# A graph layer on one core: load order, residual bias, scatter inputs and first-edge columns rearranged

## The chip, the cores and the metric

The kernel runs on one core of a Trainium2 chip. The metric is the device time of one execution in microseconds (us); lower is better. A core has TensorE (PE, with its weight loads listed apart as PEld), VectorE (DVE), ScalarE (ACT), GpSimd (POOL) and SyncE (SP), each with its own queue of instructions that run in order, and DMA queues that SP, ACT and POOL issue to. DRAM is the chip's large memory; all engines compute on the on-chip memory.

## The reference

One layer of a graph network with 625 nodes of 512 features, 20625 edges (10000 in both directions and a loop at each node, sorted by destination) and 4 relations. All is float32.

```python
h = relu(layernorm(x))                                  # x: 625 x 512
xs = h[src]
for r in range(4):
    w_r = where(edge_type == r, edge_weight, 0)
    total_msg += (xs @ W_rel[r] + b_rel[r]) * w_r[:, None]
agg = segment_sum(total_msg, dst) / maximum(segment_sum(edge_weight, dst), 1)
x1  = layer_norm(h + h @ W_self + b_self + agg, ln1)
ffn = gelu(x1 @ W_ffn1 + b_ffn1) @ W_ffn2 + b_ffn2      # 512 -> 1024 -> 512
out = x + layer_norm(x1 + ffn, ln2)
```

## The kernel before

The nodes lie in five blocks of 128 rows. One function, `gnn_layer`, holds everything as nested helpers, and its work falls into two phases.

**Phase 1** builds a table in DRAM with one row for every pair of node and relation: h of the node times W_rel, scaled and with b_rel added. The loop `for r in range(R)`, `for i in range(NB)` makes 20 steps; step c = 5 r + i calls `table_rows(r, i)` (L393): four products of 128x512 on PE (L402), one VectorE operation that scales and adds the bias (L415) into a tile called m or tr, and a store by SP (L417). Step 19 is cut in two, 384 and 128 columns, with an operation and a store each. The normalized blocks come from `x_stats` (L372) and `pre_norm` (L364), and ACT copies their transposes (`transposed`, L353). The inputs are loaded by SP in the order of the lines from L262 on: x in xs, the first relation's weights in wr, the line of edges that reach the first outer block (`load_line`), the biases.

Beside this stand three pieces of preparation, hung into the steps. (1) The edges of the two outer blocks (0 and 4) are taken as lines: `line_columns` and `line_sums` (L631, L666, VectorE) add up the weights of equal edges and give a column of weights and a column of places (tiles weight and cell); `scatter` (L684) sends one such column into a DRAM array, cells, by an indirect DMA of POOL (L685) with a short memset behind it. `load_sums` (L702, a DMA of ACT's queue at L705) reads such an array back as sums_w, 1280 KB, after all its scatters. PE then multiplies sums_w with table rows kept on chip or read back (tr): the chunk products of L1290. (2) Further edges of the outer blocks are handled through one-hot matrices: `node_hots` (L577) makes os (L580) and od (L590) on VectorE, `weighted_hots` (L594) makes ohw from os on ACT (L598), and `outer_sum` (L612) multiplies ohw and od on PE. The first three groups, `pre_hots`, are made in steps 15 to 17; there are three ohw buffers (191, 192, 193). (3) The first edges of the inner blocks' nodes are fetched into x_edges, and `first_columns` (L802) turns them with 17 small VectorE operations into rows to gather (x_row), weights (x_on) and degrees (rdeg).

At the end of phase 1 POOL adds the bias of the last layer, b2, to x in place (L1105, five blocks); the last normalization adds that xs to its output. Then the memory pool `early` is closed. The tiles of the pool `edge`, opened next, lie where those of `early` lay: eight ms buffers, es, oh and ow. So a first write to one of them waits for what last read the old tile beneath it, scatters among them.

**Phase 2** gathers table rows edge by edge: `gather` (L1143) issues an indirect DMA of POOL (L1145) into one of the eight ms buffers and a memset (L1148) as a pause, 99 times; `gather_first` does six more (L1203). In front of the first stands `after_stores` (L699), a memset on POOL (L700) that waits for the stored rows 0 to 18 and for every scatter; the two stores of row 19 are waited for by the first gather itself. ACT (L1152) and VectorE (L1170) weight and add the rows of one destination, and `edge_sum` multiplies the sums with a one-hot of the destinations, oh (L1181, four operations with two scalars each), on PE: L1195 in one float32 product, or L1192 and L1193 with a sum split in eh and el. The first tiles go straight from ms to PE. For each block follow the first normalization, the feed-forward part (`up` L917, gelu on ACT L921, `down` L935), the second normalization and the store (L986). PE products into `spin` (L1214) fill waits.

The order of phase 2 on each engine comes from a list planner, `Plan` (L76). Every operation is given to it with an engine, an assumed duration, what it comes after, the buffers it takes and gives back, a rank and a level; the planner simulates the engines and emits the operations in the order of its simulated times. The instructions then run in that order on their engine, with semaphore waits for their real inputs. Phase 1 is emitted in the order of its code.

## Time and profile before

| | us |
|---|---|
| median of 3 runs | 267.01 (266.51 to 267.12) |
| the profiled execution | 267.43 |
| its span in the trace | 265.5 |
| PE busy | 248.5 (94%) |
| POOL busy | 200.8 (76%) |
| DVE busy | 198.3 (75%) |
| ACT busy | 64.5 (24%) |

Times in the trace count from the start of the span. A row of a timeline gives start, duration, engine, line, operation, output tile <- input tiles with shapes and a count, and in brackets how long the engine idled before it and what ended that wait. Rows with SPq, ACTq or POOLq are the issue of a DMA by that engine. A group's row gives busy time in all, the mean in ns, and the idle time ahead. A float32 product of 128x512 appears as two records. Lines are those of the kernel before.

### The profile page before, as it was taken

What the parts mean: (1) busy time and instruction counts of PE and PEld (TensorE: products, weight loads), DVE (VectorE), ACT (ScalarE), POOL (GpSimd) and SP (SyncE); (2) the same over time, 40 slices, a digit from 0 to 9 for tenths busy, and PEclk for the clock granted to TensorE, in tenths of its full rate; (3) what the DMA queues carried; (4) which work ended last, traced back from release to release, by engine and by line L of the source; (5) the groups of instructions that cost most, each with busy time, mean ns of one, the idle gap of its engine ahead of it and who ended that gap; (6) DMA issues with size and microseconds to landing.
All of it is one profiled execution on the core that took longest, in us unless ns stands there. A gap on an engine that the chain in (4) does not pass through costs nothing.

```text
span 265.5 us, 3627 instructions
## 1 busy us (share of the span) xinstructions
PE 248.5 (94%) x1055; PEld 142.0 (53%) x1055; DVE 198.3 (75%) x493; ACT 64.5 (24%) x148; POOL 200.8 (76%) x408
## 2 busy tenths in 40 slices
...
GB/s 208 350 408 408 393 359 339 299 271 80 93 267 83 310 256 258 213 369 292 324 316 327 266 200 196 199 197 197 184 197 215 204 191 233 200 81 1 43 0 42
DMA packets 23848, 60.20 MB, mean 227 GB/s; under 512 B 4321, under 2 KB 8673, under 8 KB 22674
## 3 DMA queue, kind: packets, MB, share of 16 engines
...
q14 instruction: 13, 0.11, 0.1%
HBM read 50.77 MB, written 9.17 MB: 226 GB/s over the span
## 4 chain that ended last, share of the span: by engine, by line
POOL 26%; PE 24%; DVE 23%; DMA 15%; issue 7%; ACT 1%; SPq 1%; POOLq 0%; DVEq 0%; ACTq 0%
POOL ms L1145 15%; DMA ms<-table,row_i 11%; PE ps L935 8%; POOL cells L685 5%; PE ps L917 4%; PE acc L1195 4%; PE ps L402 3%; POOL zeros L1148 3%; DVE tr L415 3%; DMA wr<-in_L_gnn_W_rel_dram 3%; DVE add L1170 2%; DVE same L671 2%; DVE oc L764 2%; DMA cells<-weight,cell 2%; PE spin L1214 1%
## 5 line engine op out<-in xcount | busy, mean ns | idle before, releaser
L1145 POOL DMA_INDIRECT ms<-table,row_i x99 | 100.1, 1011 | 15.9 <-issue 12.7
L402 PE MATMUL ps<-wr,hT 128*128 128x512 f32 (+2 forms) x168 | 71.0, 576 | 1.9 <-DMA wr<-in_L_gnn_W_rel_dram 1.9
L685 POOL DMA_INDIRECT cells<-weight,cell x43 | 45.6, 1061 | 9.4 <-issue 5.6
L402 PEld LDWEIGHTS ps<-wr,hT 128*128 128x128 f32 x168 | 30.6, 190 | 35.7 <-issue 32.2
L1170 DVE SCALAR_TENSOR_TENSOR add<-ms,wgt_g,add 128x512 f32<-128x512 f32 x40 | 29.9, 750 | 17.1 <-DMA ms<-table,row_i 15.0
L917 PEld LDWEIGHTS ps<-x1T,w_sb 128*128 128x128 f32 x320 | 37.7, 192 | 6.8 <-issue 4.1
L917 PE MATMUL ps<-x1T,w_sb 128*128 128x128 f32 (+1 forms) x320 | 38.2, 275 | 1.9 <-ACT gT L921 1.9
L1152 ACT ACTIVATE add<-ms,ed 128x512 f32<-128x512 f32 x30 | 20.7, 691 | 72.0 <-DMA ms<-table,row_i 54.5
L935 PE MATMUL ps<-w_sb,gT 128*128 128x512 f32 (+3 forms) x96 | 35.9, 522 | 0.0
L598 ACT ACTIVATE ohw<-os,w 128x128 fp32r<-128x128 f32 x40 | 12.4, 388 | 66.6 <-DVE os L580 66.6
L1290 PE MATMUL acc<-tr,sums_w 128*128 128x512 f32 x60 | 28.2, 595 | 0.3 <-PE ps L440 0.3
L935 PEld LDWEIGHTS ps<-w_sb,gT 128*128 128x128 f32 (+1 forms) x96 | 16.6, 188 | 15.8 <-issue 12.6
L1195 PE MATMUL acc<-es,oh 128*128 128x512 f32 x40 | 20.9, 603 | 2.5 <-DVE es L1170 2.5
L1148 POOL MEMSET zeros<- 128x100 bf16 x99 | 19.9, 201 | 0.1
L440 PE MATMUL ps<-ws_sb,hT 128*128 128x512 f32 x40 | 18.3, 592 | 0.0
L1290 PEld LDWEIGHTS acc<-tr,sums_w 128*128 128x128 f32 x60 | 11.1, 190 | 13.2 <-issue 11.7
L921 ACT ACTIVATE gT<-ps,bf 128x128 f32<-128x128 f32 (+1 forms) x40 | 13.7, 363 | 18.0 <-PE ps L917 14.9
L1170 DVE SCALAR_TENSOR_TENSOR es<-ms,wgt_g,add 128x512 f32<-128x512 f32 x20 | 14.9, 743 | 3.2 <-DMA ms<-table,row_i 3.0
L415 DVE SCALAR_TENSOR_TENSOR tr<-ps,rx,brel_bc 128x512 f32<-128x512 f32 x15 | 11.2, 745 | 4.1 <-POOL idle L688 2.1
L612 PE MATMUL ps<-od,ohw 128*128 128x260 f32 (+13 forms) x40 | 11.1, 405 | 2.3 <-ACT ohw L598 2.3
L440 PEld LDWEIGHTS ps<-ws_sb,hT 128*128 128x128 f32 x40 | 7.5, 190 | 9.1 <-issue 9.1
L1195 PEld LDWEIGHTS acc<-es,oh 128*128 128x128 f32 x40 | 6.9, 189 | 8.1 <-DVE es L1170 4.3
...
## 6 DMA issues: line engine op xcount, KB each, us to landing
...
ms<-table,row_i POOLq DMA_INDIRECT x99, 3.8
rows<-in_rows_dram SPq DMA_DIRECT2D x1, 1536.0 KB, 13.2
```

Of the source, the lines that this page charges most:

```text
L402: nc.tensor.matmul(p_[:, :h.stop - h.start], hT[i][:, k, :], wr_sb[r][:, k, h], start=(k == 0), stop=(k == KD - 1))
L415: nc.vector.scalar_tensor_tensor(m[:, h], p_[:, :h.stop - h.start], rx[:, i, 1:2], brel_bc[:, r * D + h.start:r * D + h.stop], op0=ALU.mul ...
L440: nc.tensor.matmul(p[0], hT[i][:, k, :], ws_sb[:, k, :], start=(k == 0), stop=(k == KD - 1))
L685: s = nc.gpsimd.indirect_dma_start(out=cells[i][:, :], out_offset=bass.IndirectOffsetOnAxis(ap=cell[i][:, k:k + 1], axis=0), in_=weight[i] ...
L917: nc.tensor.matmul(pu[:, :nn], w1_sb[:, k, f * P:(f + 1) * P], x1T_b()[:, k, :nn], start=(k == 0), stop=(k == KD - 1))
L935: nc.tensor.matmul(po[h][:n, :w], box["gT"][:, f, at], w2_sb[:, f, c], start=(f == 0), stop=(f == KF - 1))
L1145: nc.gpsimd.indirect_dma_start(out=ms[j], out_offset=None, in_=table[:, :], in_offset=bass.IndirectOffsetOnAxis(ap=row_i[:, j:j + 1], axis=0))
L1148: nc.gpsimd.memset(zeros[:, :PAUSE // 2], 0.0)
L1152: nc.scalar.activation(box["sum"], ms[j], AF.Copy, scale=wgt[:, j:j + 1])
L1170: nc.vector.scalar_tensor_tensor(to, ms[j], wgt_g[:, k, q - 1:q], box["sum"], op0=ALU.mult, op1=ALU.add)
L1195: nc.tensor.matmul(acc[bs], ohs[0][:, q, :].bitcast(F32), box["sum"] if "sum" in box else ms[j], start=(k == 0), stop=last)
L1290: nc.tensor.matmul(acc[b,], sums_w[b][:, c, :], kept[(b, c) if (b, c) in kept else c], start=first, stop=last)
```

## The change

Four edits. (1) In the queue of SP, the second quarter of the first relation's weights goes ahead of the second block of x, and the rest of them ahead of the line of edges. (2) The five additions of b2 to xs go from POOL, at the end of phase 1, to VectorE: two in step 16, two in step 17, one in step 18, each behind that step's L415. (3) The tiles weight and cell, which the scatters read, are taken from a pool (`mid`) that stays open, so that no tile of phase 2 lies on them, and `after_stores` waits for the stored rows alone. (4) `first_columns` is cut into `first_rows` (6 operations, which wait for the last L415), `first_found` (5) and `first_degrees` (6). The gathers of first rows wait for `first_rows` only, the additions that use rdeg or x_on for the last step; the planner is given 1.2 us and level 0.2 for each in place of 2.4 us and level 1.5 for the whole.

```diff
@@ line 262 of before
     nc.scalar.dma_start(xs[:, 0, D // 2:], x[:P, D // 2:])
     nc.sync.dma_start(xs[:, 0, :D // 2], x[:P, :D // 2])
     load_wr(0, [(0, 1)])
+    load_wr(0, [(1, 2)])
     load_x(1, 2)
-    load_wr(0, [(1, 2)])
+    load_wr(0, [(2, 4)])
     load_line(0)
-    load_wr(0, [(2, 4)])
     load_x(2, 3)
     load_rows(brel_bc[:, :D], 0, D)
     load_x(3, NB)
@@ line 388 of before
     held = range(NL - LA * CH, NL)
     kept = {}
 
-    stored = []
+    stored, made_row = [], []
 
     def table_rows(r, i, between=None):
         c = r * NB + i
@@ line 412 of before
                 kept[OUTER[0], c] = m
         row0 = r * NP + i * P
         for p_, h in zip(p, at):
-            nc.vector.scalar_tensor_tensor(m[:, h], p_[:, :h.stop - h.start], rx[:, i, 1:2],
-                                           brel_bc[:, r * D + h.start:r * D + h.stop], op0=ALU.mult, op1=ALU.add)
+            made_row.append(nc.vector.scalar_tensor_tensor(m[:, h], p_[:, :h.stop - h.start], rx[:, i, 1:2],
+                                           brel_bc[:, r * D + h.start:r * D + h.stop], op0=ALU.mult, op1=ALU.add).ins)
             stored.append(nc.sync.dma_start(table[row0:row0 + P, h], m[:, h]).ins)
 
     begun = set()
@@ line 619 of before
         nc.gpsimd.iota(spill[-1], pattern=[[1, n]], base=P * NC * P, channel_multiplier=n,
                        allow_small_or_imprecise_dtypes=True)
         for of, name in ((place, "place"), (found, "found"), (weight, "weight")):
-            of.append(early.tile([P, n], F32, name=f"{name}_{b}"))
-        cell.append(early.tile([P, n], I32, name=f"cell_{b}"))
+            of.append((mid if name == "weight" else early).tile([P, n], F32, name=f"{name}_{b}"))
+        cell.append(mid.tile([P, n], I32, name=f"cell_{b}"))
         line_f.append(early.tile([P, 3, n + 2 * NEAR + 1], F32, name=f"line_f{b}"))
         line_key.append(early.tile([P, n + 2 * NEAR + 1], F32, name=f"line_key{b}"))
 
@@ line 697 of before
                               reason=reason)
 
     def after_stores():
-        wait_for(nc.gpsimd.memset(idle[:, :2], 0.0), [*stored[:NC - 1], *sum(scattered, [])], "rows are stored")
+        wait_for(nc.gpsimd.memset(idle[:, :2], 0.0), stored[:NC - 1], "rows are stored")
 
     def load_sums(i):
         b = lines[i][0]
@@ line 799 of before
                 out=x_edges[:, b, :, :].rearrange("p q f -> p (q f)"), out_offset=None, in_=edge_groups[:, :],
                 in_offset=bass.IndirectOffsetOnAxis(ap=x_group[:, b:b + 1], axis=0))
 
-    def first_columns():
-
-        nc.vector.tensor_copy(x_cols, x_edges[:, :, :, 0:3])
+    def first_rows():
+
+        wait_for(nc.vector.tensor_copy(x_cols, x_edges[:, :, :, 0:3]), made_row[-1:], "behind the last row")
         for f in range(2):
             nc.vector.tensor_scalar(x_step, x_cols[:, :, :, f], float(ep.gap_at), float(ep.gap), op0=ALU.is_ge, op1=ALU.mult)
             nc.vector.tensor_add(x_cols[:, :, :, f], x_cols[:, :, :, f], x_step)
         nc.vector.scalar_tensor_tensor(x_row, x_cols[:, :, 1:, 2], float(NP), x_cols[:, :, 1:, 0], op0=ALU.mult, op1=ALU.add)
+
+    def first_found():
+
         of_node = xw[:, 0, :]
         nc.vector.tensor_tensor(x_on, x_cols[:, :, 1:, 1], of_node.unsqueeze(2).to_broadcast([P, INNER, EG - 1]),
                                 op=ALU.is_equal)
@@ line 813 of before
         nc.vector.tensor_mul(x_on, x_on, xw[:, 2, :].unsqueeze(2).to_broadcast([P, INNER, EG - 1]))
         nc.vector.reduce_sum(x_found, x_on.rearrange("p b q -> p (b q)"), axis=mybir.AxisListType.X)
         nc.vector.tensor_sub(x_missing, x_missing, x_found)
+
+    def first_degrees():
+
         nc.vector.tensor_mul(x_on, x_on, x_edges[:, :, 1:, 3].bitcast(F32))
         nc.vector.reduce_sum(x_deg, x_on, axis=mybir.AxisListType.X)
         nc.vector.tensor_add(rdeg[:, 1:NB - 1], rdeg[:, 1:NB - 1], x_deg)
@@ line 998 of before
     WARM = 24
     ES = 8
     LAND = 3.6
-    HOTS_AT, SELF_AT = (15, 16, 17), 15
+    HOTS_AT, SELF_AT, ADDS_AT = (15, 16, 17), 15, (16, 17, 18)
     OHS = 3
     OW = 5
     GT = 2
@@ line 1077 of before
                     cols = degree_columns()
                 if step in DEGREE_HOTS_AT:
                     hots.append((step, degree_hots(*chunks[DEGREE_HOTS_AT.index(step)], *cols)))
+                if step in ADDS_AT:
+                    for b in range(*((0, 2), (2, 4), (4, NB))[ADDS_AT.index(step)]):
+                        nc.vector.tensor_add(xs[:, b, :], xs[:, b, :], b2_bc)
                 if step == SELF_AT:
                     for k in range(KD):
                         w_k = ws_sb[:, k, k * P:(k + 1) * P]
@@ line 1101 of before
                     total_outside = count_outside()
             later_loads(r)
         assert not columns
-        for b in range(NB):
-            nc.gpsimd.tensor_add(xs[:, b, :], xs[:, b, :], b2_bc)
         assert not pieces and len(DEGREE_HOTS_AT) == len(chunks)
     early_stack.close()
     edge = ctx.enter_context(tc.tile_pool(name="edge", bufs=3))
@@ line 1123 of before
     op = todo.op
     at_ = {}
 
-    first_ready = op("DVE", 2.4, first_columns, rank=(0.3,), level=1.5)
+    rows_of_first = op("DVE", 1.2, first_rows, rank=(0.3,), level=0.2)
+    first_ready = op("DVE", 1.2, first_found, after=[rows_of_first], rank=(0.3,), level=0.2)
+    first_ready = op("DVE", 1.2, first_degrees, after=[first_ready], rank=(0.3,), level=0.2)
 
     def read_outside():
         at_["outside"] = nc.values_load(n_out[0:1, 0:1], min_val=0, max_val=4 * P * NT)
@@ line 1228 of before
         for b in range(1, NB - 1):
             if bs == ((b, b + 1) if b < NB - 2 else (b,)):
                 for q in range(EG - 1):
-                    g_last = op("POOL", GATHER, lambda b=b, q=q: gather_first(b, q, ms), after=[g_last, first_ready],
+                    g_last = op("POOL", GATHER, lambda b=b, q=q: gather_first(b, q, ms), after=[g_last, rows_of_first],
                                 take=["ms"], lag=LAND, order=True, rank=(0, n))
-                    adds[b].append(op("DVE", 0.75, lambda b=b, q=q: add_first(b, q, ms), after=[g_last],
+                    adds[b].append(op("DVE", 0.75, lambda b=b, q=q: add_first(b, q, ms), after=[g_last, first_ready],
                                       give=[("ms", g_last)], lag=SLACK, rank=(0.3, n), level=0.05))
         for k, unit in enumerate(units):
             box, needs, got = {}, [], []
@@ line 1276 of before
         for q, b in enumerate(bs):
             half_ = slice(0, P) if len(bs) == 1 else slice(H, P) if q == 0 else slice(0, H)
             m = op("DVE", 0.72, lambda b=b, bs=bs, half_=half_: add_to(b, lambda: acc[bs], half_),
-                   after=[m], give=["acc"] if b == bs[-1] else [], rank=(0.3, n), level=1.5 if len(bs) == 1 else 0.05)
+                   after=[m, first_ready], give=["acc"] if b == bs[-1] else [], rank=(0.3, n), level=1.5 if len(bs) == 1 else 0.05)
             adds[b].append(m)
 
     def chunk_load(b, c, n):
@@ line 1339 of before
             op("PE", 0.1, read_outside, after=[t, m[b]], rank=(2, 2.365))
     for b in OUTER:
         adds[b].append(op("DVE", 0.72, lambda b=b: add_to(b, lambda: acc[b,], slice(0, P)),
-                          after=[m[b]], give=["one"], rank=(0.4,)))
+                          after=[m[b], first_ready], give=["one"], rank=(0.4,)))
 
     turned = {}
     sums_done = {}
```

The changed kernel's lines from L804 on stand 6 to 9 higher: L1290 is L1299 there, L1195 is L1204, L917 is L923, L935 is L941. Beside the planner's figures the edits change what the planner orders, on PE and ACT too. On ACT, around the end of phase 1, where cells_98 and cells_100 are the two arrays of scattered sums and the sums_w tiles what is read back from them, stood:

```order
L598 ACTIVATE ohw_191<-os_844,w_159 128x128 x4
L705 DMA sums_w_877<-cells_98 128x2560
L598 ACTIVATE ohw_192<-os_879,w_159 128x128 x4
L598 ACTIVATE ohw_193<-os_894,w_159 128x128 x4
L705 DMA sums_w_988<-cells_100 128x2560
L598 ACTIVATE ohw_191<-os_997,w_159 128x128 x4
L598 ACTIVATE ohw_192<-os_1004,w_159 128x128 x4
```

and stands now:

```order
L598 ACTIVATE ohw_191<-os_844,w_159 128x128 x4
L705 DMA sums_w_877<-cells_98 128x2560
L598 ACTIVATE ohw_192<-os_881,w_159 128x128 x4
L705 DMA sums_w_977<-cells_100 128x2560
L598 ACTIVATE ohw_193<-os_898,w_159 128x128 x4
L598 ACTIVATE ohw_191<-os_981,w_159 128x128 x4
L598 ACTIVATE ohw_192<-os_990,w_159 128x128 x4
```

The second load, which waits for the last scatters, went from behind the third group of ohw (193) to ahead of it.

On PE, between the first group of products with gathered tiles (its last one reads ms_941) and the second (ms_942 to ms_945), where od and ohw are the one-hots of the outer blocks and sums_w the scattered sums, stood:

```order
L1195 MATMUL acc_2_1034<-ms_941,oh_958 128x512
L612 MATMUL ps_79<-od_190,ohw_193 128x240 x2
L1290 MATMUL acc_954<-tr_734,sums_w_877 128x512
L1290 MATMUL acc_954<-m_837,sums_w_877 128x512
L612 MATMUL ps_79<-od_188,ohw_192 128x240 x2
L1195 MATMUL acc_2_1102<-ms_942,oh_1059 128x512
L1195 MATMUL acc_2_1102<-ms_943,oh_1059 128x512
```

and stands now:

```order
L1204 MATMUL acc_2_1041<-ms_941,oh_970 128x512
L612 MATMUL ps_79<-od_190,ohw_193 128x240 x2
L612 MATMUL ps_79<-od_188,ohw_192 128x240 x2
L612 MATMUL ps_79<-od_189,ohw_192 128x220 x2
L612 MATMUL ps_80<-od_1_185,ohw_191 128x480
L612 MATMUL ps_80<-od_1_185,ohw_191 128x220
L612 MATMUL ps_80<-od_187,ohw_191 128x200 x2
L1299 MATMUL acc_954<-tr_734,sums_w_877 128x512
L1299 MATMUL acc_954<-m_837,sums_w_877 128x512
L1299 MATMUL acc_954<-m_874,sums_w_877 128x512
L1204 MATMUL acc_2_1123<-ms_942,oh_1066 128x512
L1204 MATMUL acc_2_1123<-ms_943,oh_1066 128x512
```

Six products of od more and one more chunk product (m_874) stand ahead of the product with ms_942.

On PE at the end of phase 2, around the last two products with gathered sums (acc_1), the up products (x1T) and down products (gT) of the block before and the transposes of the last block (ow), stood:

```order
L1195 MATMUL acc_1_1774<-es_1974,oh_1827 128x512
L917 MATMUL ps_81<-x1T_1848,w_sb 128x128 x4
L917 MATMUL ps_79<-x1T_1848,w_sb 128x128 x4
L935 MATMUL ps_78<-w_sb,gT_1920 128x512 x2
L1195 MATMUL acc_1_1774<-es_2000,oh_1946 128x512
L1195 MATMUL acc_1_1774<-ms_938,oh_1984 128x512
L935 MATMUL ps_78<-w_sb,gT_1920 128x512 x6
L350 MATMUL ps_80<-ident,ow_950 128x128 x2
L350 MATMUL ps_81<-ident,ow_950 128x128 x2
L1214 LDWEIGHTS zeros
```

and stands now:

```order
L923 MATMUL ps_81<-x1T_1855,w_sb 128x128 x4
L941 MATMUL ps_80<-w_sb,gT_1922 128x512 x4
L1204 MATMUL acc_1_1779<-es_2009,oh_1953 128x512
L1204 MATMUL acc_1_1779<-ms_945,oh_1991 128x512
L941 MATMUL ps_80<-w_sb,gT_1922 128x512 x4
L1223 LDWEIGHTS zeros
L1223 MATMUL spin<-zeros 128x256
```

followed by four more such pairs of spin and then by the transposes. Two down products went ahead of the last two sums, and the five spins ahead of the transposes instead of behind.

## The prediction

> **What bounds the kernel now.** I read the page first: the line of engines under the chain of work that ended last, and the costliest groups.
>
> ```profile
> POOL 26%; PE 24%; DVE 23%; DMA 15%; issue 7%; ACT 1%; SPq 1%; POOLq 0%; DVEq 0%; ACTq 0%
> L1145 POOL DMA_INDIRECT ms<-table,row_i x99 | 100.1, 1011 | 15.9 <-issue 12.7
> ```
>
> No engine holds the chain by itself. POOL leads with the gathers of phase 2: 99 of 1.011 us (six more stand at L1203), each with a 0.2 us memset behind it, and nearly all idle time ahead of them is "issue". The table by stretches (length, then busy PE, PEld, DVE, ACT, POOL with their counts, the clock, the DMA share and GB/s) shows whether they ever wait.
>
> ```profile
> 100.00:230.00 130.00, 123.21 (x502) 71.46 (x501) 100.35 (x205) 41.66 (x86) 114.64 (x191) 1.00 0.77 239
> ```
>
> POOL is busy for 115 of these 130 us, and the rest is the 0.16 us ahead of each gather that the row above calls "issue". So the stream never waits; when it starts decides when it ends. Does its end set the kernel's end? The timeline there:
>
> ```profile
> 227.56 0.69 ACT L1152 ACTIVATE add<-ms,ed 128x512 f32<-128x512 f32 x1 [4.47 <-DMA ms<-table,row_i]
> 228.59 2.05 PE L917 MATMUL ps<-x1T,w_sb 128*128 128x128 f32 x16 [1.39 <-ACT gT L921]
> 230.75 1.14 POOL L1145 DMA_INDIRECT ms<-table,row_i  x1 [0.16 <-issue]
> 237.03 5.31 PE L935 MATMUL ps<-w_sb,gT 128*128 128x512 f32 x12
> ```
>
> At 227.56 ACT has waited 4.47 us for a gather; the gelu queued behind that add lets PE go on at 228.59, after 1.39 us of idling. From there PE is busy through the last row sum, which ends as 237.03 begins, and on. So the gathers hold the end through ACT, and PE has 1.39 us of slack there. **Model: the end moves with the stream's start, unless PE comes later than those 1.39 us allow.** The turn between the phases starts the stream:
>
> ```profile
> 81.27 4.14 DMA cells<-weight,cell
> 82.33 6.18 POOL L1105 TENSOR_TENSOR xs<-xs,rows 128x512 f32<-128x512 f32 x5
> 88.71 1.01 POOL L1145 DMA_INDIRECT ms<-table,row_i  x1
> ```
>
> The last scatter is issued at 81.27 and lands 4.14 us later, at 85.4 (this row is of the chain of waits); from 82.33 POOL adds, to 88.51; the memset at L700, whose stores and scatters are all done by then, and the first gather follow. The adds alone set 88.71.
>
> **The change part by part.** Everything is set against the profiled execution, 267.43 us around a span of 265.5; the runs' median, 267.01, is 0.42 lower.
>
> *Adds off POOL.* POOL would be free at 82.4. What is late next? The gathers read the table, so all its stores must have landed. The rows of the tile table between 60 and 90 us give that, the last for its stores from issue to landing:
>
> ```profile
> L417 SPq DMA_DIRECT2D table<-m x6: 319/320/320, 70.4 to 84.5; - x6
> DMA to landing us min/median/max: 1.9/2.3/4.9
> ```
>
> The last store is issued at 84.5. The bounds are 1.9 and 4.9, the latter the store of row 16, beside which the first load of sums (1280 KB) ran. I take 1.9, since the last store is the smallest (64 KB) and nothing so large is in flight: 84.5 + 1.9 = 86.4, the first gather starts there instead of at 88.71. Term: **-2.3**; bounds -2.3 and +0.7 (84.5 + 4.9 = 89.4).
>
> *Adds on VectorE.* Their price is that of an addition of the same shape, beside the L415 rows of phase 1's end:
>
> ```profile
> L885 DVE TENSOR_TENSOR z<-ow,rows 128x512 f32<-128x512 f32 x5 | 3.4, 687 | 0.0
> 77.20 0.75 DVE L415 SCALAR_TENSOR_TENSOR m<-ps,rx,brel_bc 128x512 f32<-128x512 f32 x1 [1.71 <-PE ps L402]
> 80.64 0.75 DVE L415 SCALAR_TENSOR_TENSOR m<-ps,rx,brel_bc 128x512 f32<-128x512 f32 x1
> 83.22 0.62 DVE L415 SCALAR_TENSOR_TENSOR m<-ps,rx,brel_bc 128x384 f32<-128x384 f32 x1 [1.83 <-PE ps L402]
> 84.11 0.35 DVE L415 SCALAR_TENSOR_TENSOR m<-ps,rx,brel_bc 128x128 f32<-128x128 f32 x1 [0.27 <-PE ps L402]
> ```
>
> Five times 0.687 is 3.4 us. Step 16's two (1.37) lie in the 1.71 us that DVE idled before 77.20. Step 17's two push row 18's L415 from 80.64 to about 82.0; its store follows, and landing the median 2.3 later it is there by 85.2, ahead of row 19's. Step 18's one lies in the 1.83 us before 83.22. The last L415 waits for PE at 84.11, with or without them. Term: **0**; without that cover, the 1.37 of step 17 at most.
>
> *Scatter inputs in memory of their own.* Here the old wait takes DVE's time too:
>
> ```profile
> 84.37 2.31 PE L612 MATMUL ps<-od,ohw 128*128 128x460 f32 x12
> 85.80 0.33 ACTq L705 DMA_DIRECT2D sums_w<-cells  x1
> 85.83 3.53 DVE L1181 TENSOR_SCALAR oh<-node_row,dst_mod,ed 128x128 f32<-128x128 f32 x4 [1.37 <-DMA cells<-weight,cell]
> L1181 DVE TENSOR_SCALAR oh<-node_row,dst_mod,ed x8: 334/340/2762, 85.8 to 97.5; 128x128 f32<-128x128 f32 x8
> 89.29 0.17 DVE L804 CAST x_cols<-x_edges 128x27 f32<-128x27 int32 x1
> 92.81 4.78 ACT L598 ACTIVATE ohw<-os,w 128x128 fp32r<-128x128 f32 x16 [13.20 <-DVE os L580]
> 93.26 1.46 PE L612 MATMUL ps<-od,ohw 128*128 128x500 f32 x4 [2.29 <-ACT ohw L598]
> ```
>
> DVE waited 1.37 us for the scatters, then took 3.53 us for four operations because one lasted 2762 ns against 340 (POOL's adds ran), then did the first columns, 17 operations from 89.29 to 92.3; only then came os, at 92.7, and ACT and PE starved behind it. After, DVE goes on at 84.5: six of the 17 (1.1), the four oh at 0.34 (1.3, with their gaps), os at about 86.9. PE's 2.29 us are over, but ACT is late next: the order puts the load that waits for every scatter ahead of ohw_193. That load left at 85.80, for 0.33; behind it the four weightings of ohw_193 run at 0.30 to 0.35 us each (16 in 4.78), to 87.5. Four of the twelve products that PE does from 84.4 need them, and PE has the eight others done at 85.7. So PE stalls about 1.1 us there (the first is ready at 86.5, the rest pace at 0.32 instead of the 0.19 of 2.31 over 12). Net -1.2.
>
> The idle gap had a second price, which the table shows in the column of the clock:
>
> ```profile
> 94.00:97.00 3.00, 2.95 (x6) 1.64 (x7) 2.98 (x11) 3.00 (x12) 2.68 (x5) 0.50 0.86 296
> 97.00:98.00 1.00, 1.00 (x5) 0.53 (x3) 1.00 (x5) 1.00 (x5) 0.84 (x2) 0.88 0.70 188
> 228.00:229.00 1.00, 0.41 (x3) 0.41 (x4) 0.71 (x1) 1.00 (x4) 0.88 (x1) 1.00 0.64 160
> ```
>
> After 2.29 us of idling the granted clock was 0.50 for 3 us and some tenths, which cost some 1.6 us; at the 1.39 us of idling at 228 it was 1.00. A stall of 1.1 should leave it, so PE gains 1.2 + 1.6 = 2.8 us in all (bounds: nothing, with a stall like the old one, and 3.9 without any). That is more than the stream's 2.3. Does the new order of products hold a buffer too long?
>
> ```profile
> 102.46 3.60 PE L1195 MATMUL acc<-ms,oh 128*128 128x512 f32 x8
> 105.73 0.95 POOL L1145 DMA_INDIRECT ms<-table,row_i  x1 [0.16 <-issue]
> ```
>
> The fifth gathered tile was read from 102.46 on, 0.9 us each (four in 3.60); its buffer serves the thirteenth gather, at 105.73 before and 103.4 after. In the order it now stands behind six more products of od (0.14 us each, scaled by width from the twelve in 2.31) and one more chunk product (0.9), 1.7 in all: 102.46 - 2.8 + 1.7 + 0.9 = 102.3. It fits by 1.1. Term: **0 beyond the stream's 2.3**.
>
> *First columns in three steps.* The same 17 operations, 3.0 us of DVE; the gathers of first rows need only the first six, which run from 84.5 to 85.6, and stand behind gathers that start at 86.4. Term: **0**.
>
> *Load order.* The start:
>
> ```profile
> GB/s 208 350 408 408 393 359 339 299 271 80 93 267 83 310 256 258 213 369 292 324 316 327 266 200 196 199 197 197 184 197 215 204 191 233 200 81 1 43 0 42
> 7.67 0.41 DVE L636 CAST line_f<-line 128x474 f32<-128x474 int32 x1 [0.42 <-DMA line<-in_edge_line_dram]
> 9.36 0.32 DVE L641 SCALAR_TENSOR_TENSOR line_key<-line_f 128x158 f32<-128x158 f32 x1
> 9.93 3.67 PE L402 MATMUL ps<-wr,hT 128*128 128x512 f32 x8 [1.89 <-DMA wr<-in_L_gnn_W_rel_dram]
> 10.54 0.69 DVE L376 BATCH_NORM_STATS2 st_x<-xs 128x6 f32<-128x512 f32 x1 [0.85 <-DMA xs<-in_x_dram]
> 11.48 0.49 DVE L366 TENSOR_SCALAR z<-xs,mv_x 128x512 f32<-128x512 f32 x1
> 13.44 0.60 PE L350 MATMUL ps<-ident,z 128*128 128x128 f32 x4
> ```
>
> PE waited for the third and fourth weights until 9.93. Without the edge line's 316 KB ahead (0.9 us at the page's second figure, 350 GB/s) they land 0.9 earlier. But the line, which DVE had at 7.67, now lands about when they did, at 9.8; DVE's 2.0 us on it (to 9.68 before) move there, and the third block's statistics (10.54 before) behind them, to 11.8. Its z is done 1.43 us after those start (10.54 to 11.97), at about 13.2, and PE transposes it no earlier, instead of at 13.44. Term: **-0.2** of a possible -0.9; the other bound is +0.6 (the line landing with the third block, 0.7 later). It shifts all of phase 1, so it adds to the stream's.
>
> *Tail.* Two of the six down products that ran behind the last row sum now run ahead of it, and 0.55 us of filler stands ahead of the last block's transposes instead of behind them.
>
> ```profile
> 240.24 0.88 DVE L881 SCALAR_TENSOR_TENSOR ow<-ow,rs_z,rows 128x256 f32<-128x256 f32 x2 [0.47 <-POOL rs_z L343]
> 242.18 0.60 PE L350 MATMUL ps<-ident,ow 128*128 128x128 f32 x4
> ```
>
> DVE has the transposes' input at 241.12, PE gets to them at 242.18: at most 1.1 us is to be had, if PE is free earlier. If PE stays busy throughout, as from 228.59, the filler costs its 0.55. In between: the first gelu no longer stands behind the add that waits, so PE has one group of up products (0.5 us, a quarter of the 2.05) more to do in its 1.39 us of idling. I take that: 0.55 - 0.5, **0**; bounds -1.1 and +0.55.
>
> Sum: 267.43 - 2.3 - 0.2 = 264.9 to 265.1, as the first gather's 86.4 holds part of the start's 0.2; 265.1 against the profiled run, less 0.42: **264.7**.
>
> **The rivals.** *R1, the tail shortens too.* For it: fewer products between the last row sum and the transposes. Against: PE was busy throughout. -1.1: 263.6.
>
> *R2, PE is the bound.* If the last scatter lands a microsecond later than 85.4, PE's stall nears the 2.29 us that lowered the clock; PE then gains nothing, only its 1.39 us of slack at 227 is left: 267.43 - 1.4 - 0.42 = 265.6. Against: a gap of 1.39 left the clock alone. By the Trainium skill ("TensorE: Matmul & The Clock Gate", Part 1: The HAM clock gate) the clock halves only after an idle window of about 3.4 us; the trace does not agree, with 2.29 us enough here. By that rule the clock's 1.6 would not be at stake at all.
>
> *R3, the sums' load collides with the last stores.* If the last scatter lands early, ACT sends its 1280 KB just ahead of row 19's stores, and they land as row 16's did. The scatters' rows, issue to landing last:
>
> ```profile
> L685 POOL DMA_INDIRECT cells<-weight,cell x14: 967/968/1427, 59.6 to 81.3; - x14
> DMA to landing us min/median/max: 2.1/2.5/4.1
> ```
>
> At the median of 2.5 the load goes at 83.8. The stores then take up to 4.9, the first gather comes at 88.7 to 89.4: 267.0 to 267.7, say 267.2. For it: that median; against: the last one took 4.14.
>
> *R4, slower: VectorE's adds hold up POOL's scatters.* One of DVE's operations took 2.76 us while POOL added, so the two do block one another. Where the adds stand now, POOL scatters. Should each add hold a scatter for its 0.687, the last lands 3.4 us later, at 88.8. The load, ohw_193 and PE follow by 3.4, the stall of 4.5 halves the clock (1.6 more), the buffer comes free at 102.3 + 5.0 = 107.3, and the thirteenth gather is 1.6 later than its 105.73: 267.43 + 1.6 - 0.42 = 268.6. It decides from 1.8 us of delay on (105.73 - 102.3 - 1.6). Against: the scatters last 968 ns at the median beside a busy DVE. The Trainium skill ("SBUF — State Buffer", SBUF: two separate sides) states that VectorE and GpSimd share a port pair held for a whole instruction, and that a VectorE operation with two inputs in SBUF counts against a GpSimd operation that reads SBUF. The add is such an operation and L415 is not, so the median above does not answer it; the 2.76 us agree with the lock. By that rule R4 could come, to the extent that a scatter reads SBUF.
>
> **How the numbers follow.** Forecast 0.52, R1 0.13, R2 0.08, R3 0.17, R4 0.10. A measurement of this kernel tells 0.2% (0.53 us) from no change. Faster: the forecast, R1, R2 and 0.04 of R3, 0.77. Same: 0.10 of R3 and 0.02 of R4, 0.12. Slower: the rest, 0.11. The range runs from R1 with 0.4 below it, 263.2, to R3's 267.2; outside are R4 (0.10), R3's upper part (0.06) and 0.04 below.
>
> **What would show it.** First gather at 86.2 to 86.4 with the last store's landing just before it; L700 not waiting past 86; PE's gap before L612's last four near 1.1 us; a clock of 1.00 from 90 to 100; a wait of PE for gelu near 226 still there; POOL at 8.9 of 10 from 98 on. Wrong: a first gather past 88 (R3), PE's gap over 2 us with a clock of 0.50 (R2), scatters above 1.5 us beside the adds (R4), or gathers with gaps after the twelfth.

## The result, and the profile after

The changed kernel takes 270.38 us (median of 8 executions, 268.55 to 274.32) against 267.15 (8, 266.51 to 268.35) for the kernel before beside it: 1.0103 times as long, 95% interval 1.0073 to 1.0133. It is slower by 2.7 us; 264.7 was predicted. A second measurement (run g2_after) gave 271.01 (270.32 to 274.65) against 268.03 (266.18 to 269.15), 1.0129 (1.0082 to 1.0176).

The profile taken with the first measurement is of its longest execution, 274.32 us, which the ratio leaves out; so the readings below are of a second profile of the changed kernel, of 271.12 us (run g2_after). Beside it was measured g1_both_again, the changed kernel with two things undone, which is needed below and stands here as the third column. Starts in us:

| | before | changed | two things undone |
|---|---|---|---|
| statistics of the third block (L376) | 10.54 | 13.27 | 9.89 |
| last L415 | 84.11 | 85.48 | 83.53 |
| first gather | 88.71 | 94.88 | 87.87 |
| thirteenth gather | 105.73 | 111.51 | 106.98 |
| last gather | 230.75 | 236.07 | 231.72 |
| last row sum done (next down product starts) | 237.03 | 242.25 | 238.07 |
| last block's transposes | 242.18 | 246.23 | 242.05 |
| end of the span | 265.55 | 268.99 | 264.44 |

The changed kernel's page has the span, the shares of the chain that ended last, and the group of the gathers:

```profile
span 269.0 us, 3610 instructions
...
PE 42%; DVE 19%; DMA 17%; POOL 13%; issue 5%; ACT 1%; SPq 1%; POOLq 0%; DVEq 0%; ACTq 0%
...
L1154 POOL DMA_INDIRECT ms<-table,row_i x99 | 98.9, 999 | 21.6 <-issue 11.9
```

POOL's share of the chain fell from 26% to 13%: the adds are gone from it, and fewer gathers lie on it. DMA's rose from 15% to 17% and PE's from 24% to 42%. The gathers take what they took (999 ns), but 21.6 us of idling stand ahead of them instead of 15.9, and POOL's part in that is one wait of 5.88 us ahead of the first.

**Where the time went first: the start.** The changed kernel's timeline, with PE's products of the first weights (L402), the 72 small memsets of GpSimd (L466, a table of constants) in one row, the cast of the edge line and the third block:

```profile
8.76 3.67 PE L402 MATMUL ps<-wr,hT 128*128 128x512 f32 x8
8.84 2.65 POOL L466 MEMSET lim<- 128x35 f32 x72
9.74 2.02 DVE L636 CAST line_f<-line 128x474 f32<-128x474 int32 x1 [1.48 <-DMA line<-in_edge_line_dram]
...
13.27 0.69 DVE L376 BATCH_NORM_STATS2 st_x<-xs 128x6 f32<-128x512 f32 x1
...
14.75 0.66 PE L350 MATMUL ps<-ident,z 128*128 128x128 f32 x4 [2.32 <-DVE rx L367]
```

The weights do come 1.17 us earlier (L402 at 8.76 instead of 9.93). The edge line comes at 9.74, as the prediction had it (9.8). But its cast takes 2.02 us instead of 0.41, the third block is 2.73 us later, and PE stands 2.32 us waiting for it: transposes at 14.75 instead of 13.44. The last L415 is 1.37 us later.

**Where it went next: the turn.** The same profile from the last L415 on, and the two large transfers that start there (size, and us from issue to landing):

```profile
85.48 0.35 DVE L415 SCALAR_TENSOR_TENSOR m<-ps,rx,brel_bc 128x128 f32<-128x128 f32 x1 [0.27 <-PE ps L402]
85.61 0.33 ACTq L705 DMA_DIRECT2D sums_w<-cells  x1
...
88.67 0.33 POOL L700 MEMSET idle<- 128x2 bf16 x1 [4.47 <-issue]
...
94.88 1.00 POOL L1154 DMA_INDIRECT ms<-table,row_i  x1 [5.88 <-DVE sum L555]
...
98.41 2.04 PE L1204 MATMUL acc<-ms,oh 128*128 128x512 f32 x2 [5.86 <-issue]
```

```profile
sums_w<-cells ACTq DMA_DIRECT2D x1, 1280.0 KB, 8.3
table<-m SPq DMA_DIRECT2D x1, 192.0 KB, 8.5
```

POOL is free early, as planned (L700 waits for stores, not for work of its own, and starts where the first gather used to). But the read-back of the sums, 1280 KB, is issued at 85.61, ahead of the last store (64 KB, issued at 85.86) and just behind the 192 KB one. The row names an operation of VectorE (L555) as what ended the 5.88 us; by the program the gather waits for the two stores of row 19, and in the trace the last of them lands at 94.08. This is R3's collision: 9.40 us from the last L415 to the first gather, 4.60 before.

The trace tells of the landing of each of these transfers by 16 events, and a wait needs all 16, so the sizes above need a closer look. Of the 192 KB store 15 events come within 1.9 us of its issue, as if no load were there; its 8.5 us are one late event. The store that the load holds up is the last one, of 64 KB: 15 of its events come 5.0 to 5.9 us after its issue (1.4 to 1.5 before), each some 0.2 us behind one of the load's own, and the sixteenth after 8.2. Without the late event the last store would have been there at 91.7; the 2.4 us from there to 94.08 are that event's. Row 18's store has a late one too, 2.4 us behind its other 15, and it has so in g1 as well, where the load has not started by then; so the load is not what makes one event in 16 late.

The longest execution shows the same two things (its cast of the edge line takes 2.72 us):

```profile
88.53 0.33 ACTq L705 DMA_DIRECT2D sums_w<-cells  x1
...
91.63 0.29 POOL L700 MEMSET idle<- 128x2 bf16 x1 [4.52 <-issue]
...
97.48 0.98 POOL L1154 DMA_INDIRECT ms<-table,row_i  x1 [5.57 <-DVE od L590]
```

PE's gap in the outer products is gone (no wait stands ahead of the thirteenth L612 product, where 2.29 us stood), but PE now runs dry 5.86 us ahead of the first gathered tile, and the granted clock falls to 0.50 (columns as in the prediction's table):

```profile
95.00:96.00 1.00, 0.00 (x0) 0.00 (x0) 1.00 (x5) 1.00 (x4) 1.00 (x2) 0.50 0.05 20
...
98.00:101.00 3.00, 2.59 (x3) 1.17 (x4) 0.00 (x0) 0.00 (x0) 2.68 (x5) 0.50 0.71 184
101.00:102.00 1.00, 1.00 (x3) 0.52 (x2) 0.00 (x0) 0.00 (x0) 0.84 (x3) 0.69 0.76 225
```

In all it is at 0.50 for 6.8 us (94.8 to 101.6), twice the 3.4 us of before.

**What was given back.** The first gather is 6.17 us late, the end only 3.44. At the tail, behind the last row sum:

```profile
242.25 3.60 PE L941 MATMUL ps<-w_sb,gT 128*128 128x512 f32 x8
...
245.46 0.88 DVE L887 SCALAR_TENSOR_TENSOR ow<-ow,rs_z,rows 128x256 f32<-128x256 f32 x2 [0.47 <-POOL rs_z L343]
...
246.23 0.60 PE L350 MATMUL ps<-ident,ow 128*128 128x128 f32 x4
```

With two down products fewer between them, the transposes follow the last row sum by 3.98 us instead of 5.15 and start as DVE delivers. That is R1's 1.1 us, nearly to the digit (1.17).

### The profile page after: what moved, and what is told of

It is laid out like the page before. It is cut to its first block, busy times and chain, and to the rows that moved or that the text cites. A ratio compares the mean times of both kernels' runs of the same rounds, so it can differ in the third digit from the quotient of the medians.

```text
span 272.2 us, 3610 instructions
## 1 busy us (share of the span) xinstructions
PE 251.2 (92%) x1055; PEld 142.6 (52%) x1055; DVE 200.2 (74%) x498; ACT 65.5 (24%) x148; POOL 194.4 (71%) x403
## 4 chain that ended last, share of the span: by engine, by line
PE 40%; POOL 20%; DVE 17%; DMA 15%; issue 5%; ACT 1%; SPq 1%; POOLq 0%; DVEq 0%; ACTq 0%
PE ps L402 24%; POOL ms L1154 15%; DMA ms<-table,row_i 12%; PE ps L941 5%; PE ps L923 4%; POOL zeros L1157 3%; DVE add L1179 3%; PE acc L1204 3%; DMA line<-in_edge_line_dram 3%; DVE z L428 2%; POOL ms L1212 2%; DVE es L1179 2%; PE add L781 1%; DVE od L590 1%; DVE line_f L636 1%
## 5 line engine op out<-in xcount | busy, mean ns | idle before, releaser
L1154 POOL DMA_INDIRECT ms<-table,row_i x99 | 98.5, 995 | 21.4 <-issue 12.9
L402 PE MATMUL ps<-wr,hT 128*128 128x512 f32 (+2 forms) x168 | 72.4, 584 | 0.6 <-DMA wr<-in_L_gnn_W_rel_dram 0.6
L685 POOL DMA_INDIRECT cells<-weight,cell x43 | 46.2, 1075 | 9.8 <-issue 5.6
L402 PEld LDWEIGHTS ps<-wr,hT 128*128 128x128 f32 x168 | 31.1, 193 | 35.2 <-issue 32.5
L923 PEld LDWEIGHTS ps<-x1T,w_sb 128*128 128x128 f32 x320 | 37.6, 192 | 5.4 <-issue 3.8
L923 PE MATMUL ps<-x1T,w_sb 128*128 128x128 f32 (+1 forms) x320 | 38.1, 275 | 0.7 <-ACT gT L927 0.4
L941 PE MATMUL ps<-w_sb,gT 128*128 128x512 f32 (+3 forms) x96 | 35.9, 522 | 0.0
L1299 PE MATMUL acc<-tr,sums_w 128*128 128x512 f32 x60 | 29.3, 608 | 0.0
L941 PEld LDWEIGHTS ps<-w_sb,gT 128*128 128x128 f32 (+1 forms) x96 | 16.7, 188 | 16.6 <-issue 14.3
L1204 PE MATMUL acc<-es,oh 128*128 128x512 f32 x40 | 21.0, 608 | 3.7 <-DVE es L1179 3.6
L1299 PEld LDWEIGHTS acc<-tr,sums_w 128*128 128x128 f32 x60 | 11.5, 195 | 12.6 <-issue 12.5
L1204 PE MATMUL acc<-ms,oh 128*128 128x512 f32 x18 | 9.7, 657 | 5.6 <-POOL zeros L1157 5.6
L415 DVE SCALAR_TENSOR_TENSOR tr<-ps,rx,brel_bc 128x512 f32<-128x512 f32 x15 | 11.2, 745 | 4.5 <-PE ps L402 2.4
L1204 PEld LDWEIGHTS acc<-es,oh 128*128 128x128 f32 x40 | 6.8, 189 | 10.5 <-DVE es L1179 7.8
```

The costliest lines, as they stand in the source:

```text
L402: nc.tensor.matmul(p_[:, :h.stop - h.start], hT[i][:, k, :], wr_sb[r][:, k, h], start=(k == 0), stop=(k == KD - 1))
L685: s = nc.gpsimd.indirect_dma_start(out=cells[i][:, :], out_offset=bass.IndirectOffsetOnAxis(ap=cell[i][:, k:k + 1], axis=0), in_=weight[i] ...
L923: nc.tensor.matmul(pu[:, :nn], w1_sb[:, k, f * P:(f + 1) * P], x1T_b()[:, k, :nn], start=(k == 0), stop=(k == KD - 1))
L941: nc.tensor.matmul(po[h][:n, :w], box["gT"][:, f, at], w2_sb[:, f, c], start=(f == 0), stop=(f == KF - 1))
L1154: nc.gpsimd.indirect_dma_start(out=ms[j], out_offset=None, in_=table[:, :], in_offset=bass.IndirectOffsetOnAxis(ap=row_i[:, j:j + 1], axis=0))
L1204: nc.tensor.matmul(acc[bs], ohs[0][:, q, :].bitcast(F32), box["sum"] if "sum" in box else ms[j], start=(k == 0), stop=last)
```

## The experiments

Two theories, and both could hold. *Start*: the new load order brings the edge line under GpSimd's memsets. *Collision*: the read-back of the sums leaves ahead of row 19's stores. The rivals were R4 (adds of VectorE), the new order on PE, and the new memory itself.

One thing limits the reading. In the first four sets of runs every kernel, that of before too, took some 40 us more (before: 301 to 319 us), with stretches of a granted clock of 0.50 that lie elsewhere in each profile, so their medians tell little; I read distances between events in their traces, and times from the last set, which ran like the first measurement.

### Set 1: the kernel again, and each theory's cause taken away

e0_after_again is the changed kernel. e1_order_undone is it with the old load order:

```diff
     load_wr(0, [(0, 1)])
-    load_wr(0, [(1, 2)])
     load_x(1, 2)
-    load_wr(0, [(2, 4)])
+    load_wr(0, [(1, 2)])
     load_line(0)
+    load_wr(0, [(2, 4)])
```

e2_order_alone is the kernel before with the new load order (the same lines the other way). e3_sums_behind_stores is the changed kernel with the second read-back waiting for row 19's two stores as well:

```diff
-                 scattered[i][:-1], "all cells are there")
+                 [*scattered[i][:-1], *(stored[-2:] if i else [])], "all cells are there")
```

> The changed kernel as it is, for a second profile; the one shown took 274.3 us where the others took 268.6 to 271.0. Three theories for the loss of 1.0%. START: the new load order lets the second block of x and the line of edges come late, so phase 1 ends late. COLLISION: the read-back of the second sums (1280 KB), issued just ahead of the last row's second store, delays that store and with it the first gather. CHANCE: the first profile's late start was that one execution's own. All expect 269.5 to 270.5. START expects the last L415 at 86 to 88.5 (84.1 before), CHANCE at 84 to 84.5; COLLISION expects 6 us or more from the last L415 to the first gather, where 2.4 would do.

> The changed kernel with the load order of before; the three other edits stay. START: the last L415 is back at 84 to 84.5 and the kernel gains 2 to 4 us on the changed one (266 to 268). COLLISION alone: it stays at 269.5 to 270.5, the first gather 6 us or more behind the last L415. Both together: 267 to 268, the last L415 at 84.2 and the first gather at 90 or later.

> The kernel before with the new load order alone. START: 1 to 4 us slower than before, all of it there by the end of phase 1. COLLISION: no loss, 266.8 to 267.4 (my prediction gave this edit -0.2).

> The changed kernel, with the second read-back of sums waiting for both stores of the last row as well. On ACT it then stands behind the third weighting of one-hots (ohw_193) instead of ahead of it; nothing else moves. COLLISION: the last store lands 1.9 to 2.5 us after its issue, the first gather starts 2.4 to 3 us behind the last L415, and the kernel gains 3 us or more on the changed one. START alone: no gain (within 0.5 us).

Ratios to the kernel before on that chip: e0 1.0162 (1.0061 to 1.0262), e1 1.0065 (0.998 to 1.0151), e2 0.9959 (0.9832 to 1.0085), e3 0.9961 (0.9853 to 1.0069). Only e0 is told from 1. The traces say more. From the last L415 to the first gather: e0 7.25, e1 7.48, e3 3.43, e2 4.13. So the collision comes with the other edits, whatever the load order, and holding the load back removes it. The start comes with the load order: statistics of the third block at 13.24 (e0), 13.33 (e2, nothing else changed) and 13.08 (e3), but 10.66 with the old order (e1); cast 1.84, 1.88, 2.22 and 0.41 us.

### Set 2: both undone, and the memsets moved

e1b and e3b repeat e1 and e3; e4_both joins their edits; e5_memsets_first is e3 with the two calls that write the memsets ahead of the first block's normalization:

```diff
+        set_limits(0)
+        set_limits(1)
         pre_norm(0, x_stats(0))
...
-        set_limits(0)
-        set_limits(1)
         line_columns(0, nc.gpsimd)
```

> The same kernel as e1_order_undone, once more, since the chip of the first four runs took 308 to 319 us for the kernel before and no difference under 1.5% can be told there. START (now from four profiles: with the new load order the third block's statistics begin at 13.1 to 14.5 instead of 10.5 to 10.7): 1.2 to 2.7 us under the changed kernel's 269.9. COLLISION: first gather still 7 us or more behind the last L415, against 4.6 before, so not under 267.

> The same kernel as e3_sums_behind_stores, once more. COLLISION: first gather 3.4 us behind the last L415 (7.3 without the edit on that chip), so 3 to 4 us under the changed kernel's 269.9: 266 to 267. CHANCE or START alone: 269 to 270.

> The changed kernel with both: the load order of before, and the second read-back of sums behind the last row's stores. If START and COLLISION are the whole loss, this gains what my prediction had for the other edits, 2 to 3 us on the kernel before: 264 to 265.2. If another of the edits costs time too, it stays at 266 or above.

> e3_sums_behind_stores with GpSimd's 72 small memsets (L466) ahead of its first block statistics' follow-up instead of behind the second block's. With the new load order these memsets run beside VectorE's cast of the edge line, which then takes 1.8 to 2.7 us instead of 0.41 in all four profiles. If GpSimd's memsets hold the cast up, it is back at 0.41 and the third block's statistics start at 11.6 to 12, 1.4 earlier, and the kernel gains 0.7 to 1.4 on e3b. If the cast is slow for another reason (the line still landing), it stays at 1.8 or more and nothing is gained.

e1b gave 311.84 us beside 311.1 for the kernel before (no interval); e3b 0.9893 (0.9818 to 0.9968), e4 0.9869 (0.9807 to 0.9932), e5 0.9722 (0.9631 to 0.9813). The turn agrees with set 1 (7.59 in e1b; 4.15, 3.78 and 4.14 where the load is held back). The start does not: e1b has the old order and yet

```profile
8.31 2.92 DVE L636 CAST line_f<-line 128x474 f32<-128x474 int32 x1 [0.57 <-DMA line<-in_edge_line_dram]
8.33 2.65 POOL L466 MEMSET lim<- 128x35 f32 x72
...
12.75 0.68 DVE L376 BATCH_NORM_STATS2 st_x<-xs 128x6 f32<-128x512 f32 x1
```

The cast and the memsets start within 0.02 us of each other, and the cast ends 0.25 us after them, at 11.23. In e4 it is 2.81. So "load order" was not the whole cause; it is the meeting with the memsets. In e5 they run before, and the victim is another operation, the first block's normalization, 1.48 us instead of 0.62:

```profile
2.90 2.65 POOL L466 MEMSET lim<- 128x35 f32 x72
...
4.47 1.48 DVE L366 TENSOR_SCALAR z<-xs,mv_x 128x256 f32<-128x256 f32 x2
...
12.00 0.69 DVE L376 BATCH_NORM_STATS2 st_x<-xs 128x6 f32<-128x512 f32 x1
```

### Set 3: the adds, the memory, and the memsets once more

e0c repeats the changed kernel. e6_adds_on_pool is e4 with the five additions back on POOL. e7_memory_alone is the kernel before with edit 3 and nothing else: no instruction changes its place. e8_memsets_behind_cast is e4 with the first memset waiting for the cast. The edits of e6, e7 and e8:

```diff
-                if step in ADDS_AT:
-                    for b in range(*((0, 2), (2, 4), (4, NB))[ADDS_AT.index(step)]):
-                        nc.vector.tensor_add(xs[:, b, :], xs[:, b, :], b2_bc)
...
         assert not columns
+        for b in range(NB):
+            nc.gpsimd.tensor_add(xs[:, b, :], xs[:, b, :], b2_bc)
```

```diff
-            of.append(early.tile([P, n], F32, name=f"{name}_{b}"))
-        cell.append(early.tile([P, n], I32, name=f"cell_{b}"))
+            of.append((mid if name == "weight" else early).tile([P, n], F32, name=f"{name}_{b}"))
+        cell.append(mid.tile([P, n], I32, name=f"cell_{b}"))
...
-        wait_for(nc.gpsimd.memset(idle[:, :2], 0.0), [*stored[:NC - 1], *sum(scattered, [])], "rows are stored")
+        wait_for(nc.gpsimd.memset(idle[:, :2], 0.0), stored[:NC - 1], "rows are stored")
```

```diff
-        nc.vector.tensor_copy(line_f[i], line[i][:, 0:3, :])
+        cast = nc.vector.tensor_copy(line_f[i], line[i][:, 0:3, :])
+        if i == 0:
+            wait_for(set_limits(0), [cast.ins], "behind the cast")
+            set_limits(1)
```

> The changed kernel as it is again, beside the three others on their chip. Whatever the chip: third block's statistics at 13 us or later, first gather 7 us or more behind the last L415, and 0.5 to 1.6% slower than before.

> e4_both with the five additions back on GpSimd at the end of phase 1. My prediction gave the additions 2.3 us of gain on GpSimd; in e4_both the first gather stood 6.9 us behind the last scatter's start, where the kernel before, with the additions, had 7.4. If stores, not additions, set the first gather: 6.9 to 7.5 again, row 18's L415 back at one step (3.4 us) behind row 17's instead of 4.6, and a time within 0.3% of e4_both. If the additions do cost what I said: 2 us or more over e4_both.

> The kernel before with the third edit alone: weight and cell in memory of their own, and the memset ahead of the gathers not waiting for scatters. The order on every engine is that of before. If the wait of VectorE for the scatters (1.37 us) and TensorE's 2.29 us behind it are what the change wins, TensorE's gap ahead of the second group of outer products shrinks and the kernel gains 0.5 to 2 us. If VectorE's operation is held by GpSimd's additions anyway (2.76 us for one of 0.34), it gains under 0.5.

> e4_both with the first of GpSimd's 72 memsets waiting for VectorE's cast of the edge line. If the memsets hold the cast up when they start first (as in e1b and e4: memsets first by 0.1 us or in the same 0.02, cast 2.8 to 2.9), the cast is 0.41 in every profile and the third block's statistics start at 10.5 to 11 instead of 12.5; 1 us or more under e4_both. If not, the cast stays long.

e0c 1.0208 (1.0133 to 1.0283); e6 308.77 us beside 308.32 (no interval); e7 0.9897 (0.9843 to 0.9951), e8 0.9971 (0.9932 to 1.001). e7's timeline at the turn:

```profile
100.94 6.18 POOL L1105 TENSOR_TENSOR xs<-xs,rows 128x512 f32<-128x512 f32 x5
102.57 0.33 ACTq L705 DMA_DIRECT2D sums_w<-cells  x1
103.28 0.35 DVE L415 SCALAR_TENSOR_TENSOR m<-ps,rx,brel_bc 128x128 f32<-128x128 f32 x1 [0.27 <-PE ps L402]
...
107.07 0.17 POOL L700 MEMSET idle<- 128x2 bf16 x1
...
110.51 0.99 POOL L1145 DMA_INDIRECT ms<-table,row_i  x1 [3.27 <-DVE rdeg L819]
```

Edit 3 alone brings the collision: the load leaves 0.71 us ahead of the last L415, not 1.69 behind as before, and the first gather, with POOL free of its adds at 107.12, waits until 110.51. That is 7.23 us behind the last L415. By the trace's landing events, one of the 16 landings of the last scatter is late in the kernel before: 1.30 us behind the last L415 where the other 15 land 0.45 ahead of it; a 16 KB instruction fetch, on a queue of its own, runs on one DMA engine just then. In e7 all 16 are there 1.09 us ahead of the last L415. So in the kernel before the load was held behind the stores by one late landing (late by as much in f1, f2 and e2, the other profiles with its memory). That the fetch makes it late is read from their place in time, not tried. What makes the scatters land 0.6 us earlier with edit 3 is open. Nor does e7's time fit: with the collision in it, it came out 1% under the kernel before. That isn't explained; like the other times of these sets it is not used here.

e6 bounds what the adds are worth: its first gather comes 4.05 us behind the last L415, e4's 3.78; against the last scatter 7.44 and 6.91. Five additions of 6.2 us in all taken off POOL bring the gathers forward by 0.3 to 0.5 us between these two profiles, and that is less than the eight profiles with the adds on VectorE and the load held back differ among themselves (3.4 to 4.3). What POOL gained was in part lost at the stores. On VectorE two of the additions put row 18's store 1.1 us nearer to row 19's. In e4 SP then takes 0.86 us to issue the last store and its last landing event comes 2.98 us behind the last L415; in e6 0.32 and 2.16.

In e8 the cast takes 0.41 us, as expected, but the next operation is hit instead, and the third block's statistics come at 12.83, not at 10.5 to 11:

```profile
8.37 0.41 DVE L638 CAST line_f<-line 128x474 f32<-128x474 int32 x1 [0.79 <-DMA line<-in_edge_line_dram]
8.82 2.86 DVE L642 TENSOR_SCALAR line_up<-line_f 128x316 f32<-128x316 f32 x1
8.84 2.66 POOL L466 MEMSET lim<- 128x35 f32 x72 [0.63 <-DVE line_f L638]
```

### Set 4: no memsets, and the kernel before held back

f1_before is the kernel before. f2_before_sums_behind is it with the held-back load of e3. f3 and f4 write the 72 constants on ScalarE, in step 5, in the old load order (f3, from e4) and in the new one (f4, from e3):

```diff
-                nc.gpsimd.memset(lim[:, a, j0:j], float(limits[j0][a]))
+                nc.scalar.activation(lim[:, a, j0:j], node_row[:, j0:j], AF.Copy, bias=float(limits[j0][a]), scale=0.0)
```

> The kernel before as it is, for a second profile. Two mechanisms were found in the variants: a VectorE operation that meets GpSimd's 72 memsets waits for their end (2.3 us), and the read-back of the second sums, when it is issued ahead of the last row's stores, delays them by 4 to 6 us. The one profile of before showed neither. If they belong to the change: again the third block's statistics at 10.5 to 10.7 and the first gather 4.6 us behind the last L415. If that profile was a lucky one (memsets began 0.16 us behind the cast, the last scatter landed 1.8 us late): statistics at 12.5 to 13, or the first gather 6 to 7.5 behind the last L415, or both.

> The kernel before with one edit: the second read-back of sums waits for the last row's stores too. The order on every engine is that of before. If before meets the collision in most executions, 0.5 to 1.2% faster than before; if it does not, within 0.3%.

> e4_both (load order of before, read-back behind the stores) with the 72 constants of the tile lim written by ScalarE in step 5 instead of by GpSimd's memsets at the start. If the memsets starve VectorE: the cast 0.41, line_up 0.34 and the third block's statistics at 10.4 to 10.8 (12.5 in e4), PE's third transposes at 13.0 to 13.4, and 0.3 to 0.8% under e4's 0.987 of before.

> The same with the new load order. The cast 0.41 at 9.6 to 10, the third block's statistics at 11.5 to 12, its transposes at 13.2 to 13.8. This sets the load order alone against f3 with the memsets out of the way. My prediction's term for it was -0.2 (z at 13.2 instead of 13.44): if right, f4 is within 0.3% of f3; if the late second block of x costs by itself, f4 is 0.3% or more slower.

f1 307.33 us and f3 311.95 us beside 309.95 (no interval); f2 1.0213 (1.0113 to 1.0314), f4 1.0164 (0.9933 to 1.0395). That f2, which changes a single wait by 0.4 us (load 2.11 behind the last L415 instead of 1.66 in f1, first gather 4.12 instead of 4.13), comes out 2% slower shows how little the times of these four sets decide. In the traces even the kernel before is hit in f1 (the cast starts 0.45 us ahead of the memsets, and the operation behind it, which starts 0.01 us ahead of them, is caught):

```profile
7.76 0.41 DVE L636 CAST line_f<-line 128x474 f32<-128x474 int32 x1
...
8.20 2.84 DVE L637 TENSOR_SCALAR line_up<-line_f 128x316 f32<-128x316 f32 x1
8.21 2.65 POOL L466 MEMSET lim<- 128x35 f32 x72
...
12.19 0.69 DVE L376 BATCH_NORM_STATS2 st_x<-xs 128x6 f32<-128x512 f32 x1
```

Without memsets nothing is; f3 (old order) and f4 (new):

```profile
8.30 0.41 DVE L636 CAST line_f<-line 128x474 f32<-128x474 int32 x1 [0.66 <-DMA line<-in_edge_line_dram]
...
10.74 0.69 DVE L376 BATCH_NORM_STATS2 st_x<-xs 128x6 f32<-128x512 f32 x1 [0.43 <-DMA xs<-in_x_dram]
...
13.22 0.60 PE L350 MATMUL ps<-ident,z 128*128 128x128 f32 x4
```

```profile
9.69 0.41 DVE L636 CAST line_f<-line 128x474 f32<-128x474 int32 x1 [1.63 <-DMA line<-in_edge_line_dram]
...
11.61 0.69 DVE L376 BATCH_NORM_STATS2 st_x<-xs 128x6 f32<-128x512 f32 x1
...
13.09 0.66 PE L350 MATMUL ps<-ident,z 128*128 128x128 f32 x4 [0.65 <-DVE rx L367]
```

The load order by itself moves the statistics from 10.74 to 11.61 and the transposes from 13.22 to 13.09: what the prediction had (11.8, and 13.2 for 13.44). Its harm is that the line then meets the memsets: in all seven profiles with the new order and the memsets in their old place the cast took 1.84 to 2.72 us; of nine with the old order, six were caught and three not (before, e1, g1).

### Set 5: both undone, timed

g1_both_again is e4, g2_after the changed kernel.

> The same kernel as e4_both, with the changed kernel beside it. On a chip that runs the kernel before in 267: 265 to 266.5, since the first gather comes 3.4 to 4.2 us behind the last L415 (seven profiles with the read-back behind the stores) instead of 4.1 to 4.6 (before), and TensorE's gap in the outer products is gone; not the 264.7 of my prediction, whose first gather was 2.3 behind the last L415. On a slow chip: 0.5 to 2% under the changed kernel.

> The changed kernel beside it. First gather 7 us or more behind the last L415, the read-back issued ahead of the last row's second store, as in all five profiles of kernels with the change's read-back. On a chip that runs the kernel before in 267: 269 to 271.

In this set the kernel before takes 268.03 us (17 executions), g1 267.11 (12), 0.9986 times (0.9957 to 1.0015), and g2 1.0129 as told above. Undoing the two brings back the whole loss. But the 265 to 266.5 expected of g1 did not come: what is left of the change gains nothing that can be measured (at most 0.4%). The new order of products on PE is in g1 too and was not tried by itself. Why nothing is gained is shown in g1's timeline; below it the landings of row 18's and row 19's stores, and how long SP took to issue these three (min, median and max in ns, then the first and the last issue; before: 319/319/320):

```profile
87.25 0.33 ACTq L705 DMA_DIRECT2D sums_w<-cells  x1
...
87.87 0.98 POOL L1154 DMA_INDIRECT ms<-table,row_i  x1 [0.81 <-DVE od L590]
...
94.61 2.04 PE L1204 MATMUL acc<-ms,oh 128*128 128x512 f32 x2 [4.01 <-issue]
...
105.68 2.74 PE L1204 MATMUL acc<-ms,oh 128*128 128x512 f32 x6
...
106.98 0.95 POOL L1154 DMA_INDIRECT ms<-table,row_i  x1 [2.92 <-PE acc L1204]
```

```profile
table<-m SPq DMA_DIRECT2D x1, 256.0 KB, 4.5
...
table<-m SPq DMA_DIRECT2D x1, 192.0 KB, 3.6
...
table<-m SPq DMA_DIRECT2D x1, 64.0 KB, 3.2
...
L417 SPq DMA_DIRECT2D table<-m x3: 319/320/1421, 82.0 to 83.9; - x3
```

The first gather comes 4.34 us behind the last L415, 0.26 less than before. With no load beside them 15 of the 16 landing events of row 18's store still come by 83.98 and the last one at 86.46; the issue of the last store takes 1.42 us, and it lands from 86.4 to 87.1. Then the load, issued at 87.25, runs beside the first gathers instead of the stores: the first one's last packet lands at 94.4, 6.5 us after its issue, against 93.5 before (4.8 us after) and 98.2 in g2 (3.3 us, with nothing beside it). So PE, free of its outer products since 90.6, gets its first gathered tile at 94.61, where it had it at 94.77 before. It has idled for 4.01 us, and the clock is at 0.50 for 6.8 us. The product that frees the thirteenth gather's buffer then starts at 105.68, and that gather waits 2.92 us.

## Why the prediction was wrong

*The model held, its slack did not.* The stream of gathers never waits and takes what it took: first to last 141.2 us in g2, 142.0 before. In g1, where PE came late (thirteenth gather), it took 143.9.

*Adds off POOL, -2.3: the step that failed.* The prediction put the last store's landing at 1.9 us, "since the last store is the smallest (64 KB) and nothing so large is in flight". Something so large was: R3's load. In g2 the 64 KB store landed 5.0 to 5.9 us after its issue but for one event, and that one after 8.2. R3 was the right mechanism with too small a chance (0.17, because the last scatter had taken 4.14 us before). Its price, the largest landing of before, 4.9 us, was near what the load itself costs; it lacked the late sixteenth event (2.4 us) and the time from a landing to the gather. By the Trainium skill ("DMA: Bandwidth & Descriptors", Queues, rings and completion order) a DMA engine takes turns between the queues that it has work for, and drains a whole packet, typically 9 to 17 descriptors, before it switches. The load has eight records of 10 KB for each of 16 engines; if a record is one descriptor, that rule lets the whole share go ahead of a store behind it. The trace agrees for the 64 KB store: but for one engine the load's records lie from 86.6 to 90.8, and the store's from 90.3 to 91.3. It does not where the late events come from: there records of the load and of the 192 KB store alternate from 91.2 to 93.4.

Even without the collision the term was wrong. The stores of g1 took 3.2 to 4.5 us, not 1.9 to 2.3, and 0.8 us more, which the prediction put at nothing, pass from the last landing to the gather (from 87.1 to 87.87; 106.74 to 107.54 in e4). Worked anew, 83.9 for the last issue, 3.2 and 0.8 give 87.9. The term is -0.26 (4.60 to 4.34).

*Why R3 came about: scatter inputs in memory of their own.* The prediction priced edit 3 by the waits it takes away on DVE, ACT and PE, and took the last scatter's 4.14 us as a property of it. That was one late event of 16; the 15 others had landed within 2.4 us, near the median of 2.5 that R3 named. The scatter's landing fell to 2.1 us in g1 and g2, and e7 showed that edit 3 alone sends the load ahead of the stores. What the prediction gave the edit did come too: PE's gap of 2.29 us went, altogether where 1.1 was expected to remain. But the next tile was not there, so the clock's 1.6 us were not gained: it is at 0.50 for 6.8 us instead of 3.4.

*The buffer "fits by 1.1": failed in g1.* The estimate, 102.3, assumed that PE goes on at full clock; PE idled 4.01 us instead. The product came at 105.68, 3.4 later, and the gather 2.92 late. In g2 the late first gather hid it (thirteenth 16.63 behind the first).

*Load order, -0.2: failed, with the right figures.* All that was worked out from rows came true where no memsets run (f4: 11.61 and 13.09 against 11.8 and 13.2). What was overlooked is in the timeline of before, right behind the cast of 7.67:

```profile
7.83 2.85 POOL L466 MEMSET lim<- 128x35 f32 x72
...
8.11 0.34 DVE L637 TENSOR_SCALAR line_up<-line_f 128x316 f32<-128x316 f32 x1
```

The cast started 0.16 us ahead of the memsets and was not held, nor was line_up, which starts inside their run. The prediction moved the cast to 9.8 without asking what runs on POOL there; cost in g2, 1.31 us at the transposes (14.75 against 13.44) and 1.37 at the last L415. The price that it did see for such a meeting (2.76 us for an operation beside POOL's adds) it used for R4 alone, and it was the same thing: that operation ends at 88.59, POOL's five adds at 88.51. So the price is the rest of POOL's run, not a fixed sum. By the Trainium skill ("SBUF — State Buffer", SBUF: two separate sides) whichever of the two engines starts first holds the shared ports for its whole instruction; the cast is indeed blocked, but for the rest of a run of 72 instructions that start 37 ns apart (2.65 us), not for one of them.

*Adds on VectorE, 0: right for VectorE, wrong for the stores.* Row 18's L415 is 1.15 us later against the last one (2.32 instead of 3.47 ahead; 1.37 expected), and the adds hold nothing else up. But the prediction had row 18's store land ahead of row 19's, and in g1 and g2 its last event comes 2.4 us behind its other 15, after 15 events of row 19's 192 KB store; the issue of the last store takes 1.4 us there instead of 0.32, and e6 against e4 puts 0.8 us on it. That the shift of row 18 causes this rests on these profiles, not on a timed run. R4 was not seen: the last scatter of g2, which an addition overlaps by 0.24 us, took 0.96 us and landed in 2.1.

*First columns, 0: right.* The first six end at 86.95 in g2, eight us ahead of the first gather.

*Tail, 0: R1's case came,* 1.17 us in g2 and 1.17 in g1 (3.98 from the last row sum to the transposes in both). It stood within the bounds.

In sum, for g2 against before: start +1.4, turn +4.8 (the collision and the late event), of which 0.9 comes back in the stream and 1.9 behind the last gather (R1's 1.2 among it): +3.4 in the span. What the two chief terms cost the end one by one was not timed in runs like the first measurement's; together they are the 3.9 us between g2 and g1.
